# A cross-attention kernel with adapter tokens on one core: another hand-laid order of all operations and another choice of engines

## The chip, the cores and the metric

The kernel runs on one core of a Trainium2 chip. The core has five engines with a queue each: TensorE (PE, matrix products; its weight loads are shown apart as PEld), VectorE (DVE), ScalarE (ACT), GpSimd (POOL) and SyncE (SP), which here issues nearly all DMAs. Each engine works through its queue in program order and waits on semaphores for the others. SBUF holds the working data, PSUM the results of PE in banks. The metric is the device time of one execution in microseconds, from repeated runs.

## The reference

x is 2 x 2048 x 640 in f32, the context 2 x 128 x 384: 124 text keys and T = 4 adapter tokens. With 8 heads of 80:

```python
query = hidden_states @ Wq
keyt = enc @ Wk
valt = enc @ Wv
hs = _mha(query, keyt, valt)
ca_q1 = jnp.einsum('btc,th->bch', ca, Wq_ca)
ca_q1 = ca_q1[:, indices, :]
ca_hs1 = _mha(ca_q1, residual, residual)
ca_q2 = ca_hs1 @ Wq
ca_k2 = ca @ Wk_ca
ca_v2 = ca @ Wv_ca
ca_hs2 = _mha(ca_q2, ca_k2, ca_v2)
out = hs + ca_hs2
out = out @ Wout + b_out
out = out + residual
```

So there is a text attention over 124 keys, and a second branch that attends from the adapter tokens over all 2048 rows of x (the rows `indices` choose), and once more over the four tokens. Their sum goes through Wout, with bias and residual.

## The kernel before

The rows of x are taken as 8 blocks of 512 (four to a batch entry: `x_load`, `queries`, `yz_block`) and, for the attention, as UNITS = 16 units of two tiles of 128 rows (`text(m)`). For a unit, PE multiplies queries and keys (`sc`), DVE takes the maxima (`m`), ACT the exponentials (`p`) and their sums, POOL or DVE multiplies by the reciprocal sums `r`, DVE transposes in blocks (`eb`), and the result goes out to DRAM (`kept`) and comes back transposed (`pT`); then PE multiplies by the values (`ph`) and by Wout (`po`), and DVE adds the parts to the row tile with bias (`x_more`, `last_rows`), which is stored. Units in BY_SUMS = (0, 1, 2, 3, 4, 6, 7) use f32 products in a form that saves multiplications (`text_out_fast`); the other nine use three f32r products with weights split into a rounded top, a rest and a mixed part (`wout_top`, `wout_low`, `wout_mix`; inputs `ks`).

The adapter branch runs beside this for each of the two batch entries. It first takes maxima over all rows (`s` on PE, 128 x 2048 at a time, and `mx` on DVE), then the exponentials (`ea` on ACT) and the products `acc`; `pt_acc`, `prod`, `s2f`, `p`, `p2t` and `pt_p` are its second softmax over the tokens and what makes of it the weights that join the text probabilities.

A head has 80 columns, and what goes beyond the first 64 of each pair of heads is kept apart as a rest. For the keys (`keys`, L824) the fifth chunk is rounded to f32r and to its rest by ACT (`k_parts<-k_rest`) and DVE, written to DRAM (`k_away`), read back in another layout by four DMAs (marks `krest`) and cast by ACT to `krest`. The score matmuls of the first unit read first `kmain` and `q`, then `krest` and `rests`. The scratch tile of this chain is one of three weight buffers (room `weights`).

What sets the order is neither a scheduler nor the language. Every part of the work is a generator that yields operations (`Do`), each with its allowed engines, the operations it must follow, and the buffers it takes and frees (`Room`). All generators are tasks with a number. `Desk.run` (L190) reads the text table `ORDER` (L75 on) entry by entry: a task's number, and a letter where the engine is chosen (a for ACT, v for DVE, g for POOL). An entry issues the next operation of that task. The order of the table is thus the order in each engine's queue. Semaphore waits follow from the data.

In the profile's rows L221 is the matmul of `Desk`, L225 its warm-up matmul, L229 its transpose, L236 every vector, scalar and GpSimd operation, and L246 every DMA; so rows are told apart by tile names.

Of the kernel before, what the change touches and what calls it, by code (L numbers as in the profile page):

```python
# [14 lines left out]
P = 128  # L15
# [52 lines left out]
class Desk:  # L68
# [12 lines left out]
    158 159v 158 158 158 9 36 160 162v 18 12 36 163a 12 13 36 117 123 158 17 154 158 158 158 154 154 39 161 123
    17 117v 161 165g 154 161 117v 171 175 17 161 166g 161 164 18 164 164 17 18 117g 36 164 117g 154 154 164 117g
    164 161 18 176a 164 36 164g 161 16 36 18 18 167g 171 177 16 164 16 16 16 18 36 178a 117v 117 18 43 16 36 16g
    171 181 161 117g 18 18 180 164 168g 180 36 182a 16 17 180 117g 179 180 36 179 16 171 183 16g 174 185 184a 18
    180 18 180 18 36 172 186 36 174 18 17 17 179 18 179 174 188 170 187 187 19 20 21 161 21 187 187 172 192 187
    20 189 190 21 187 36 43 36 179 179 21 173 203 203 203 191 191 36 193 191 173 204 169 103 203 191 180 36 180g
    203 191 19 21 203 21 194g 180 36 19 200 209 20 21 195g 19 36 19 191 21 39 102 210a 191 19 21 21 36 19 191
    212 200 213 211 19g 205 211 212 17 196g 20 214a 203 19 212 197g 211 212 36 200 215 211 212 180 203g 201 212
    191 20 19 212 21 216a 21 19g 21 36 20 20 21 212g 211 211 21 206 217 217 36 22 23 24 24 202 24 200 218 217
    217 24 206 222 219a 203 217 36 22 223 24 217 203 36 24 47 22 22 22 208 228 226 202 202 22 24 207 229 24 44  # L90
# [159 lines left out]
def kernel(  # L250
# [58 lines left out]
    late = {}  # L309
# [991 lines left out]

    def front_rooms():

        yield Do("NONE", lambda: None, ["late"])
        t = late["pool"].tile([P, 2, 4 * P], F32R, tag="rests", name="rests")
        rest_tiles.extend(t[:, i].rearrange("p (g n) -> p g n", g=4) for i in range(2))
        rests.grow(2)
# [1059 lines left out]
```

## Time and profile before

| | us |
|---|---|
| runs before: median of three (lowest to highest) | 564.55 (564.24 to 566.42) |
| profiled execution, first to last instruction | 562.1 |
| PE busy | 549.2 |
| DVE busy | 402.2 |
| ACT busy | 276.3 |
| POOL busy | 208.1 |

The profile is of one execution. Its span is taken from the first to the last instruction; the time of a run is the whole execution on the device. The page lists busy time by engine and by group of equal instructions; the list of waits says which engine stood idle for what; a table of windows gives busy time in chosen stretches; a timeline has the instructions in order of their start, with the idle time before each in brackets and what ended it. A group's mean is its busy time over its count, and operations on one engine overlap at their edges by some tens of nanoseconds.

### The profile page before, as it was taken

The numbers are of one execution on the slowest core, as the hardware profiler recorded it, in microseconds if no ns is written. First come the engines' busy times: TensorE is split into PE (matmuls) and PEld (weight loads), VectorE is DVE, ScalarE is ACT, GpSimd is POOL, SyncE is SP. The second block draws the span as 40 slices with busy tenths as digits, with TensorE's granted clock in tenths as the row PEclk, the third lists the DMA queues.
The fourth block names the chain that finished last, engine by engine and source line by source line (L and its number), as shares of the span: only waits on it lengthen the run. The fifth ranks groups of instructions, "written<-read, shape, count | busy, mean of one in ns | idle before, by whom it ended". The sixth has DMA issues, their size and how long they took to land.

```text
span 562.1 us, 17332 instructions
## 1 busy us (share of the span) xinstructions
PE 549.2 (98%) x7338; PEld 337.8 (60%) x7338; DVE 402.2 (72%) x621; ACT 276.3 (49%) x752; POOL 208.1 (37%) x206
## 2 busy tenths in 40 slices
PE   9999999999999999999999999999999899999997
PEld 8563455556555655455365445455554477989796
DVE  2457999999996564589999998655735886449542
ACT  3122645445338898886524524589878432111200
POOL 7002625344424522013559364512424830441040
PEclk9999999999999999999999999999999989999999
DMA  8994759774876899446558895859865367977533
GB/s 258 244 175 121 163 123 166 163 159 142 170 199 155 183 251 180 136 160 176 177 126 247 226 232 133 255 149 254 244 172 177 74 124 215 264 215 195 160 123 129
DMA packets 151549, 101.38 MB, mean 180 GB/s; under 512 B 86476, under 2 KB 130012, under 8 KB 151472
## 3 DMA queue, kind: packets, MB, share of 16 engines
q1 hardware_dynamic: 150704, 99.88, 69.5%
q8 instruction: 58, 0.95, 0.8%
q0 software_dynamic: 768, 0.40, 0.4%
q14 instruction: 19, 0.16, 0.1%
HBM read 61.34 MB, written 38.90 MB: 178 GB/s over the span
## 4 chain that ended last, share of the span: by engine, by line
PE 82%; DVE 7%; DMA 5%; ACT 2%; issue 2%; SPq 1%; DVEq 0%; ACTq 0%
PE po L221 23%; PE pq L221 23%; PE acc L221 7%; PE sc L221 6%; PE s L221 6%; PE ph L221 5%; PE pq_first L221 3%; PE pyz L221 3%; DVE mx L236 2%; ACT p L236 1%; DMA bias<-in_L_xattn_b_out_dram 1%; PE pk L221 1%; PE unread L225 1%; ACT ea L236 1%; PE pv L221 1%
## 5 line engine op out<-in xcount | busy, mean ns | idle before, releaser
L236 DVE TENSOR_REDUCE mx<-s 128x4 f32<-128x2048 f32 x48 | 109.2, 2275 | 2.9 <-PE s L221 2.8
L236 POOL TENSOR_TENSOR p<-p,r 128x992 f32<-128x992 f32 x29 | 53.8, 1856 | 141.1 <-DVE r L236 135.0
L236 ACT ACTIVATE ea<-s 128x2048 f32<-128x2048 f32 x48 | 90.4, 1884 | 25.6 <-PE s L221 25.3
L236 ACT ACTIVATE p<-sc,m 128x124 f32<-128x124 f32 x256 | 89.5, 374 | 25.7 <-DVE m L236 25.7
L236 ACT ACTIVATION_READ_ACCUMULATOR p<-sc,m 128x1 f32 x256 | 55.5, 217 | 0.0
L221 PE MATMUL pq<-xt,wq_sb 128*32 128x256 f32 x896 | 54.3, 381 | 0.6 <-DVE q L236 0.6
L236 DVE TENSOR_REDUCE m<-sc 128x4 f32<-128x496 f32 x64 | 40.6, 662 | 13.9 <-PE sc L221 13.7
L221 PE MATMUL acc<-ea,y_sb 128*32 128x384 f32 (+2 forms) x768 | 50.1, 383 | 0.0
L221 PE MATMUL ph<-pT,vpad 128*32 128x256 f32 x768 | 45.8, 380 | 0.8 <-DMA out_dram<-x_more 0.3
L236 DVE STREAM_TRANSPOSE eb<-p 128x1024 f32<-128x1024 f32 x32 | 39.5, 1233 | 4.5 <-POOL p L236 3.3
L221 PEld LDWEIGHTS pq<-xt,wq_sb 128*32 128x32 f32 x896 | 27.5, 110 | 22.9 <-issue 5.5
L221 PEld LDWEIGHTS sc<-kmain,q 64*128 64x128 f32 x512 | 31.8, 187 | 11.6 <-issue 8.4
L221 PE MATMUL pq<-xt,wq 128*32 128x512 f32 x320 | 38.8, 595 | 0.0
L221 PE MATMUL po<-wout_sums,hs 128*32 128x320 f32 x448 | 35.4, 438 | 3.5 <-DVE x_more L236 2.9
L221 PE MATMUL sc<-kmain,q 64*128 64x124 f32 x512 | 37.5, 283 | 0.1
L221 PE MATMUL po<-wout_sb,hs 128*32 128x320 f32 (+1 forms) x452 | 36.4, 434 | 0.7 <-DVE prod L236 0.6
L221 PE MATMUL po<-wout_low,ks 128*128 128x320 f32 x204 | 35.7, 308 | 0.0
L221 PEld LDWEIGHTS ph<-pT,vpad 128*32 128x32 f32 x768 | 24.4, 110 | 18.6 <-issue 2.6
L236 POOL TENSOR_TENSOR last_rows<-last_rows,bias 128x640 f32<-128x640 f32 x10 | 17.0, 1697 | 44.7 <-DMA last_rows<-in_x_dram 44.7
L221 PE MATMUL po<-wout_top,ks 128*128 128x320 f32 x180 | 32.5, 311 | 0.0
L221 PEld LDWEIGHTS acc<-ea,y_sb 128*32 128x32 f32 x768 | 21.1, 109 | 17.3 <-issue 8.6
L221 PEld LDWEIGHTS po<-wout_low,ks 128*128 128x128 f32 x204 | 31.3, 188 | 0.0
(232 smaller groups left out, 951.4 us busy)
## 6 DMA issues: line engine op xcount, KB each, us to landing
kept<-eb SPq DMA_DIRECT2D x32, 512.0 KB
pT<-kept SPq DMA_DIRECT2D x48, 256.0 KB
landing<-away SPq DMA_DIRECT2D x60, 128.0 KB
xi<-in_x_dram SPq DMA_DIRECT2D x28, 256.0 KB
x_more<-in_x_dram SPq DMA_DIRECT2D x17, 320.0 KB
out_dram<-x_more SPq DMA_DIRECT2D x16, 320.0 KB
last_rows<-in_x_dram SPq DMA_DIRECT2D x15, 320.0 KB
out_dram<-last_rows SPq DMA_DIRECT2D x14, 320.0 KB
```

Source lines behind the costliest of these rows:

```text
L221: self.pin(self.nc.tensor.matmul(out[strip], lhsT[:, strip], rhs, **kw))
L225: self.pin(self.nc.tensor.matmul(out, zeros, zeros, start=True, stop=True))
L236: return lambda *args, **kw: self.pin(getattr(engine, what)(*args, **kw))
```

## The change

The whole table `ORDER` is replaced, so that every engine's queue is laid out anew. Of the table, its first two lines of before stand here for all; of the code, the core:

```diff
     ORDER = """
-    2 4 4 0 2 36 0 0 2 0 0 2 0 0 2 0 0 2 0 0 2 2 124 2 4 2 0 128a 0 2 0 6 6 6 2 125 4 6 130a 126 4 131a 127 4 4
-    132a 6 133v 2 3 4 6 3a 2 15 3 6 3a 15 15 3 6 3v 3 7 7 8 8 7 8 11 7 7 15 0 8 135a 0 134a 7 5 8 7 7 15 9 7
...
@@ -2224,6 +2216,25 @@
+    def mixing(mix, top, low, after, marks):
+
+        def first():
+            if desk.engine == "ACT":
+                desk.a_activation(mix(), raw(low()), AF.Identity, scale=UP)
+            else:
+                mixed(mix(), raw(top()), raw(low()))
+
+        op = yield Do(("DVE", "ACT"), first, after)
+
+        def second():
+            if op.ran == "ACT":
+                minus(mix(), raw(top()), raw(mix()))
+
+        yield Do(("NONE", "POOL", "DVE"), second, marks=marks)
...
-    def stored(m, k, u, added):
+    def stored(m, k):
 
         b, st = tiles(m)[k]
-        t, i, _ = xr_of[m][k]
-        cols = slice(*spans[u])
-        yield Do(
-            "SP", lambda: dma(out[b, st * P : (st + 1) * P, cols], t[:, cols]), added,
-            frees=[(rows, i)] if u == 2 else [],
-        )
+        for u in (2,) if m < UNITS - 1 else (0, 1):
...
+            yield Do(
+                "SP", store, added,
+                frees=lambda: [(rows, xr_of[m][k][1])] if u == 2 else [],
+            )
```

The other edits give an operation's buffers free with the operation itself (`frees`, `grows`) rather than in a statement behind it, begin the stores of a unit with the unit, and put the two steps of a mixed part into one helper. The stores and the operations are the same ones. Lines move up by five: the matmul is L216 and the vector operations L231 in the change.

PE does the same products. On the other engines, counting instructions: DVE 607 to 617, ACT 498 to 503, POOL 211 to 203, SP's DMAs 427 in both. Among what changes engine: the multiplication of `p` by `r` (POOL 29 to 20, DVE 3 to 12), the subtractions that make `wout_low` (DVE 4 to 0, POOL 1 to 5), some additions for `x_sums` (POOL 24 to 20, DVE 4 to 8) and those of the bias (POOL 21 to 18).

First place: ACT's queue in the setup, ahead of the first exponentials. `k_parts<-k_rest` is the first step of the chain of the keys' rest, `krest<-k_parts` its last; the `vpad` copies take the products `pv` of the values from PSUM. Before:

```order
L236 ACTIVATE cop<-ca_150,low_c 128x384
L236 CAST k_parts<-k_rest 128x248
L236 ACTIVATE yz_0_509<-pyz_0_0_510,ones 128x512
...
L236 COPY vca<-pvca 128x2x64
L236 COPY vca<-pvca 128x16 x2
L236 COPY vpad_107<-pv_0_620 124x4x64
L236 COPY vpad_107<-pv_0_620 124x2x16 x2
L236 CAST krest<-k_parts 128x992
L236 COPY vpad_108<-pv_1_693 124x4x64
L236 COPY vpad_108<-pv_1_693 124x2x16 x2
L236 CAST rests<-first_rests 128x512 x2
```

and now:

```order
L231 COPY vca<-pvca 128x2x64
L231 COPY vca<-pvca 128x16 x2
L231 COPY vpad_107<-pv_1_653 124x4x64
L231 COPY vpad_107<-pv_1_653 124x2x16 x2
L231 CAST k_parts<-k_rest 128x248
L231 CAST krest<-k_parts 128x992
L231 COPY vpad_108<-pv_1_708 124x4x64
L231 COPY vpad_108<-pv_1_708 124x2x16 x2
L231 CAST rests<-first_rests 128x512 x2
```

The first step, which had many rows between it and the last, now stands right ahead of it, behind the copies of `pv_1_653`. On PE that product is the third from last of the values; behind it come `pv_0_667`, one `s`, `pv_1_708`, one `s`, the `kmain` half of the first scores and then their `krest` half, as in before.

The same chain in SP's queue, before:

```order
L246 DMA wout_sb<-in_L_xattn_Wout_dram 64x4x640
L246 DMA k_away<-k_parts 128x2x248 x2
L246 DMA k_parts<-k_away 32x4x248
L246 DMA away_618<-first_rests 256x1x256
L246 DMA v_638<-vca 128x192
L246 DMA k_parts<-k_away 32x4x248 x3
L246 DMA first_rests<-away_618 32x4x256 x4
```

and now:

```order
L241 DMA away_476<-first_rests 256x1x256
L241 DMA first_rests<-away_476 32x4x256 x4
L241 DMA k_away<-k_parts 128x2x248 x2
L241 DMA xi_2_553<-in_x_dram 32x64x32
L241 DMA xi_2_553<-in_x_dram 32x16x16 x2
L241 DMA k_parts<-k_away 32x4x248 x2
L241 DMA v_616<-vca 128x192
L241 DMA k_parts<-k_away 32x4x248 x2
```

The rests of the first queries now go out and come back ahead of the keys' chain, and three loads of x stand between its write and its reads.

Second place: DVE's queue behind `prod` of the second batch entry, ahead of the last phase. Before:

```order
L236 TENSOR_TENSOR prod<-pt_acc_1_5786,r_1_1_5790 128x3x96
L236 TENSOR_TENSOR wout_low<-wout_sb,wout_top_5736 128x640
L236 TENSOR_TENSOR wout_low<-wout_sb,wout_top_5694 128x640
L236 TENSOR_TENSOR wout_low<-wout_sb,wout_top_5690 128x640
L236 TENSOR_TENSOR wout_low<-wout_sb,wout_top_5692 128x640
L236 TENSOR_TENSOR wout_mix_5827<-wout_top_5694,wout_low 128x640
L236 TENSOR_TENSOR wout_mix_5828<-wout_top_5735,wout_low 128x640
L236 TENSOR_REDUCE s2f<-prod 128x8x3 x3
L236 TENSOR_REDUCE m_1_5837<-s2f 128x24
L236 TENSOR_TENSOR p_1_5732<-s2f,m_1_5837 128x96
L236 TENSOR_TENSOR x_more<-x_more,po_1_5840 128x320
```

and now:

```order
L231 TENSOR_TENSOR prod<-pt_acc_1_5747,r_1_1_5751 128x3x96
L231 TENSOR_REDUCE s2f<-prod 128x8x3 x3
L231 TENSOR_REDUCE m_1_5785<-s2f 128x24
L231 TENSOR_TENSOR p_1_5698<-s2f,m_1_5785 128x96
L231 TENSOR_REDUCE r_1_5700<-p_1_5698 128x24
L231 RECIPROCAL r_1_5700<-r_1_5700 128x24
L231 TENSOR_TENSOR p2t_5699<-p_1_5698,r_1_5700 128x3x8x4
L231 TENSOR_REDUCE m_15_0_5818<-sc_15_0_5800 128x4
L231 TENSOR_REDUCE m_15_1_5819<-sc_15_1_5801 128x4
L231 TENSOR_REDUCE m_14_0_5775<-sc_14_0_5757 128x4
L231 TENSOR_SCALAR ks_5821<-ph_2_5836 128x512
```

The splits of Wout (`wout_low`, `wout_mix`) are gone from between `prod` and `s2f`. The five subtractions stand in POOL's queue, behind the masks of the token rows, and DVE's four mixes come some ten rows further on than what is shown.

More of the change, by code (lines that the diff above doesn't have):

```diff
@@ L81 @@
[L81 to L90, printed above, removed]
@@ L1302, in front_rooms @@
     def front_rooms():
[L1304 removed]
+        yield Do("NONE", lambda: None, ["late"], grows=[(rests, 2), (landing, 1)])
         t = late["pool"].tile([P, 2, 4 * P], F32R, tag="rests", name="rests")
         rest_tiles.extend(t[:, i].rearrange("p (g n) -> p g n", g=4) for i in range(2))
[L1307 removed]
         landing.tile = late["pool"].tile([P, 4, 2 * P], F32, tag="landing", name="landing")
[L1309 to L1310 removed]
+        yield Do("NONE", lambda: None, [("rest", 0, i) for i in range(2)], grows=[(sums, 1), (halves[0], 1)])
         t = xrow.tile([P, 2 * P * NCH * 2], F32, tag="xr", name="x_sums")
@@ L1575, in scores @@
                     return q4, ea_tile(e[0], f"ea_{b}_{j}_{v}", 512), e[0]
-                op = yield Do("PE", scores, [("cop", b)], needs=[(quad, 1), (eas, 1)])
+                st = pieces(v)[-1][0]
+                ends_ = j == 1 and 512 * (v + 1) == CAD * (st + 1) and st % 4 == 3
+                op = yield Do(
+                    "PE", scores, [("cop", b)], needs=[(quad, 1), (eas, 1)],
+                    frees=(lambda st=st: [(zops, room_of["zop", b, st // 4])]) if ends_ else (),
+                )
                 q4, e, i = op.value
@@ L1587, in adapter @@
                 if j == 1 and 512 * (v + 1) == CAD * (st + 1) and st % 4 == 3:
-                    zops.give(room_of["zop", b, st // 4])
+                    late["ps_"]=0
         yield Fork(second(b))
@@ L2188, in add @@
                     desk.v_tensor_tensor(t, t, po[:, :HALF], ALU.add)
-                op = yield Do("DVE", add, [op.at], frees=[(banks, s)] if end else [])
+                op = yield Do(
+                    "DVE", add, [op.at], frees=[(banks, s)] if end else [], marks=[("added", m, i, n, k)],
+                )
                 at = [op.at]
-                key = (m, i, 2)
-                ends.setdefault(key, []).append(op.at)
-                if len(ends[key]) == 4:
-                    yield Fork(stored(*key, ends[key]))
         for n, steps in enumerate(chains):
@@ L2237, in hidden_parts @@
         )
-        def scaled():
-            if desk.engine == "ACT":
-                desk.a_activation(cols("mix"), cols("low", True), AF.Identity, scale=UP)
-            else:
-                mixed(cols("mix"), cols("top", True), cols("low", True))
-        op = yield Do(("DVE", "ACT"), scaled)
-        both = op.ran == "ACT"
-        yield Do(
-            ADDS if both else "NONE", lambda: both and minus(cols("mix"), cols("top", True), cols("mix", True)),
-            marks=[("hs mix", m, c0)],
-        )
+        yield from mixing(lambda: cols("mix"), lambda: cols("top"), lambda: cols("low"), [("hs low", m, c0)], [("hs mix", m, c0)])
     def out_part(m, i, u, hs):
@@ L2304, in text @@
         yield Fork(probabilities(m))
+        for k in range(2):
+            yield Fork(stored(m, k))
     begin = desk.begin
```

174 lines of the change are left out of this document (86 added, 88 removed), and 7 rows, old and new, of the table ORDER.

## The prediction

> **What bounds the kernel now.** I read the page first, then the list of what TensorE (PE) waits for, then a table by stage, and last the timelines at the two places where the new order differs most.
>
> ```profile
> span 562.1 us, 17332 instructions
> PE 549.2 (98%) x7338; PEld 337.8 (60%) x7338; DVE 402.2 (72%) x621; ACT 276.3 (49%) x752; POOL 208.1 (37%) x206
> ```
>
> The columns are busy us, share of the span and count. PE is busy for 98% of the span, so no reordering can win much unless it also removes matmuls, and this one removes none. All that an order can win is PE's idle time, 562.1 - 549.2 = 12.9 us, and what a lowered clock costs. The next list says where the larger part of it is (target of the wait, us in all, times, longest).
>
> ```profile
> PE po L221 <- DVE x_more L236: 2.9, 1, 2.9
> PE s L221 <- DVE mx L236: 1.1, 2, 0.8
> PE po L221 <- DVE prod L236: 0.6, 1, 0.6
> ```
>
> One wait of 2.9 us stands out; the others are fractions of a microsecond, spread over the program. The stages show how near the next engine is to PE:
>
> ```profile
> 57.00:165.00 108.00, 107.23 (x1644) 58.69 (x1648) 102.88 (x127) 52.56 (x206) 48.41 (x38) 1.00 0.74 162
> 165.00:260.00 95.00, 94.82 (x1439) 51.31 (x1427) 59.90 (x98) 81.03 (x186) 28.32 (x24) 1.00 0.71 172
> 260.00:335.00 75.00, 72.77 (x1031) 37.75 (x1031) 72.13 (x78) 31.81 (x121) 43.35 (x38) 1.00 0.75 200
> 335.00:430.00 95.00, 94.37 (x1477) 51.68 (x1473) 57.94 (x97) 68.19 (x151) 29.68 (x22) 1.00 0.70 196
> 430.00:455.00 25.00, 21.48 (x313) 11.13 (x307) 21.13 (x32) 13.92 (x21) 21.89 (x18) 0.93 0.53 131
> ```
>
> After the stretch and its length come the busy us of PE, weight loads, DVE, ACT and POOL, then the granted clock. DVE is nearly full in 57 to 165 (102.88 of 108) and 260 to 335 (72.13 of 75), ACT in 165 to 260 (81.03 of 95). The one stage where PE loses much is 430 to 455: 21.48 of 25 us busy, at a mean clock of 0.93. Its end, and the setup before 57, are where I expect the change to act.
>
> **The change, part by part.** The working starts from the profiled execution. The measured runs' median of 564.55 us is 2.45 us above its span of 562.1; I carry that difference over unchanged.
>
> *First place: the drain before the last phase.* In the order of before, DVE does the Wout splits ahead of the adapter's second softmax:
>
> ```profile
> 439.29 0.46 DVE L236 TENSOR_TENSOR prod<-pt_acc,r 128x288 f32<-128x288 f32 x1
> 439.66 5.51 DVE L236 TENSOR_TENSOR wout_low<-wout_sb,wout_top 128x640 fp32r<-128x640 f32 x4
> 445.10 2.10 DVE L236 TENSOR_TENSOR wout_mix<-wout_top,wout_low 128x640 fp32r<-128x640 f32 x2
> 447.13 1.66 DVE L236 TENSOR_REDUCE s2f<-prod 128x24 f32<-128x192 f32 x3
> 449.29 0.47 DVE L236 TENSOR_TENSOR x_more<-x_more,po 128x320 f32<-128x320 f32 x1
> 451.30 1.07 DVE L236 TENSOR_TENSOR p2t<-p,r 128x96 f32<-128x96 f32 x1
> ...
> 438.91 1.16 PE L221 MATMUL sc<-kmain,q 64*128 64x124 f32 x16
> 440.40 1.28 PE L221 MATMUL po<-wout_sums,hs 128*32 128x320 f32 x16
> 441.50 1.05 PE L221 MATMUL ph<-pT,vpad 128*32 128x256 f32 x16
> 449.82 1.66 PE L221 MATMUL po<-wout_sums,hs 128*32 128x320 f32 x16 [2.85 <-DVE x_more L236]
> 453.04 1.52 PE L221 MATMUL pt_p<-rows,p2t 128*32 128x512 f32 x12 [0.49 <-DVE ks L236]
> ...
> 450.60:454.00 3.40, 2.91 (x25) 1.18 (x20) 3.30 (x7) 0.95 (x3) 3.32 (x2) 0.50 0.73 153
> ```
>
> The PSUM bank that `po` needs is freed by the x_more addition, and that stands behind 5.51 + 2.10 + 1.66 us of other DVE work. PE idles 2.85 us, then 0.49 us more, and in 450.60 to 454.00 it runs at a clock of 0.50: 2.91 us of busy time do 1.45 us of work. The place loses 2.85 + 0.49 + 1.45 = 4.8 us. In the changed order `wout_low` is no longer on DVE (five subtractions go to POOL), the mixes come later, and s2f to p2t follow `prod` at once. p2t then comes, behind the end of `pt_acc` at 438.98, 0.8 us later with `prod` (439.75), and then the 1.66 us of s2f, the 1.07 of p2t and four small steps of about 0.26 each: 4.6 us. In the changed order PE has two score products and two `ph` between `pt_acc` and `pt_p`; one score product takes 440.40 - 438.91 = 1.49 us here and one `ph` at most 1.05, so 2 x 1.49 + 2 x 1.05 = 5.1 us at most. The two are about even, and no `po` stands behind the splits: the long wait goes. What is late next: `pt_p` (up to 0.7 us), the matmuls behind ACT's copy of `rows` (0.5), and two `po` that wait for `ks` (0.3), 1.5 us together. None reaches 2.85 us, so the clock should stay. **Gain 4.8 - 1.5 = 3.3 us**, between 1 (if the new waits come to 3.8: one of the old size, 2.85, and one more) and 4.8.
>
> *Second place: the rest of the keys in the setup.* This speaks against the change. The rounded rest of K is written to DRAM and read back in another layout (k_parts to k_away to k_parts), then cast to `krest`, which the score matmuls read:
>
> ```profile
> 38.00 0.40 ACT L236 CAST k_parts<-k_rest 128x248 fp32r<-128x248 f32 x1 [5.36 <-PE pk L221]
> 41.61 0.40 DVE L236 TENSOR_TENSOR k_parts<-k_rest,k_parts 128x248 fp32r<-128x248 f32 x1
> 42.07 1.07 SPq L246 DMA_DIRECT2D k_away<-k_parts  x2
> 45.28 0.32 SPq L246 DMA_DIRECT2D k_parts<-k_away  x1
> 51.03 0.48 SPq L246 DMA_DIRECT2D v<-vca  x1
> 51.56 1.42 SPq L246 DMA_DIRECT2D k_parts<-k_away  x3
> 51.61 0.55 ACT L236 COPY vpad<-pv 124x256 f32<-124x256 f32 x3 [0.64 <-PE pv L221]
> 56.43 1.02 ACT L236 CAST krest<-k_parts 128x992 fp32r<-128x992 f32 x1 [4.28 <-DMA k_parts<-k_away]
> 57.36 0.54 ACT L236 COPY vpad<-pv 124x256 f32<-124x256 f32 x3
> 58.25 1.14 ACT L236 CAST rests<-first_rests 128x512 fp32r<-128x512 f32 x2 [0.35 <-DMA first_rests<-away]
> ...
> 49.66 5.05 PE L221 MATMUL pv<-w_v,ctxT 128*32 128x320 f32 x72
> 57.72 0.50 PE L221 MATMUL s<-zop,cop 32*128 32x512 f32 x4 [0.82 <-DVE mx L236]
> 59.07 0.65 PE L221 MATMUL sc<-krest,rests 64*128 64x124 f32 x8
> ```
>
> In before the chain starts with the cast at 38.00, 21 us ahead of its user at 59.07, and no time is lost. In the changed order that cast stands on ACT behind the copies of the third `pv` from the end, so it cannot start before PE has finished that product. That is the second of the three in the row at 49.66, so it ends at 49.66 + 2 x 5.05 / 3 = 53.0. From there PE's program is the same as before up to the `krest` half, which before took 59.07 - 53.0 = 6.1 us, with the 0.82 us wait for `mx` in it. The new chain from the same instant: copies 0.55, cast 0.40, subtraction 0.40, write to first read 45.28 - 42.07 = 3.21, the issues of four reads and the `v` load among them 0.32 + 1.42 + 0.48 = 2.2, last issue's end to cast 56.43 - 52.98 = 3.45 (52.98 is 51.56 + 1.42), krest 1.02, copies 0.54, first half of rests 0.57. Sum 12.3 us. **PE waits 12.3 - 6.1 = 6.2 us.** Little runs beside it: DVE can do one more `mx` and then stands at an operand sum whose buffer the same chain frees, and SP is in order. The bounds: if a read lands as the write does, 45.28 - 43.14 = 2.14 us behind the last issue and not 3.45, and the one `mx` (2.28 us, below) is won back later in a stage where DVE is the fuller engine, 6.2 - 1.3 - 2.3 = 2.6 (the write's second issue ends at 42.07 + 1.07 = 43.14); if the x loads now issued between write and read (three, and in before two such cost SP 4.69 us) hold the reads up by one of them, 6.2 + 2.3 = 8.5.
>
> ```profile
> 60.91 2.28 DVE L236 TENSOR_REDUCE mx<-s 128x4 f32<-128x2048 f32 x1
> 28.43 4.69 SPq L246 DMA_DIRECT2D xi<-in_x_dram  x2
> ```
>
> The clock is a cost of its own here. Behind the 2.85 us wait it was 0.50 for 3.4 us and 1.45 us of work was lost; a wait twice as long should bring the same, but DVE gets the lost time as a lead in a stage where it is short. I take 0.7, with 0 and 1.45 as ends. The Trainium skill, page "TensorE: Matmul & The Clock Gate", section "Part 1: The HAM clock gate", says that one idle window of about 3.4 us puts the clock to half until a busy window has passed, and that the window runs freely. By it a wait of 6.2 us cannot escape, and the sum would be some 0.8 us higher. The trace agrees as to the stretch (3.4 us at 0.50), though here a wait shorter than a window sufficed. For the read-back the skill's "DMA: Bandwidth & Descriptors", "Anatomy of one DMA", gives about 2.0 us fixed cost; with it twice, in place of the two row-based landings, the sum would be about 1.6 us lower. The landings of 2.14 and 3.45 us here decide.
>
> *Third: engines changed elsewhere.* Nine more `p` multiplications run on DVE instead of POOL.
>
> ```profile
> L236 POOL TENSOR_TENSOR p<-p,r 128x992 f32<-128x992 f32 x29 | 53.8, 1856 | 141.1 <-DVE r L236 135.0
> L236 DVE TENSOR_TENSOR p<-p,r 128x992 f32<-128x992 f32 x3 | 3.5, 1180 | 0.0
> L236 DVE TENSOR_TENSOR wout_low<-wout_sb,wout_top x4: 812/1372/2192, 439.7 to 443.0; 128x640 fp32r<-128x640 f32 x4
> ```
>
> They add 9 x 1.18 = 10.6 us to DVE and take 9 x 1.86 = 16.7 from POOL, nearly all within the stages 165 to 260 and 335 to 430, where DVE is idle for 35 and 37 us. Neither is on PE's path, so I count nothing; were that cover gone, each would cost its 1.18. The last row shows DVE's same subtraction taking 0.81 to 2.19 us while POOL works: the two engines hold each other up. Fewer of these beside POOL's large operations may help in 260 to 335, where PE loses 75 - 72.77 = 2.2 us. The stage 57 to 165 gets a little more for DVE to do (one more addition for `x_sums` and one for `zop`, from POOL) with only 5 us of room. I take -1.0 for both stages together, between +1 and -2.5 (all of 260 to 335 and some of the rest). The stores begun under other marks, the rooms freed inside the operation and the common `mixing` helper issue the same DMAs and vector operations; nothing.
>
> Sum: 562.1 + 6.2 + 0.7 - 3.3 - 1.0 = 564.7; with 2.45 around it **567.2 us**.
>
> **Rivals.** (a) *The setup wait is absorbed and the change wins.* If DVE sets the pace in 57 to 165, PE's loss at `krest` is only what DVE loses: the chain of 2.6 with no clock loss. With the full gain of the drain and of the lock, 562.1 + 2.6 - 4.8 - 2.5 = 557.4, or 560 us. For it: DVE's 102.88 of 108. Against: PE is 107.23 of 108 there, so it has no lead to give. It decides where the wait at `krest` is below 3.5 us. (b) *The setup is worse.* Reads behind x loads, full clock loss and nothing won by the lock: 562.1 + 8.5 + 1.45 - 2 = 570, or 572.5 us. For it: SP's order and DVE's fullness behind the wait, which then runs late against `mx` again. (c) *It evens out.* The chain costs 3.5 us with little clock loss, and drain plus lock win 3.5 to 4: about 564.5 us. That the order isn't what the table says is no rival, as the operations stand in it one by one.
>
> **How the numbers follow.** The forecast, that the setup wait is about 6 us and is not made good: 0.45. (a) 0.2, (b) 0.2, (c) 0.15. The range takes in (a) and (b) but for their outer tails: 559.5 to 573. A measurement of this kernel can tell about 0.5% from no change, 561.7 to 567.4. Faster: (a), 0.2. Slower: (b) and somewhat under half of the forecast, 0.4. Same: the rest, 0.4.
>
> **What would show it.** In the changed profile PE should have one wait of 4 to 8 us at `sc<-krest` near 60 us, with ACT's krest cast idle on the read of k_parts, and the granted clock near 0.5 behind it; the row for 430 to 455 should have no wait above 1 us and a clock of 1.00. If the first wait is under 3 us the chain was sized wrongly; if the last phase still begins with a 3 us wait, the drain was; if PE loses over 3 us in 57 to 165 behind the setup, it is DVE that was misjudged.

## The result, and the profile after

| | before | after |
|---|---|---|
| runs: median (lowest to highest) | 564.89 us (564.24 to 566.42) | 571.9 us (571.36 to 572.58) |
| profiled execution, first to last instruction | 562.1 us | 570.6 us |
| mean granted TensorE clock in it | 0.997 | 0.990 |

The ratio is 1.0109, with a 95% interval of 1.007 to 1.0149: the new order is slower by about 1%. (The quotient of the two medians is 1.0124, inside the interval; in the table of the experiments too the ratio need not be the quotient of the medians beside it.) Forecast were 567.2 us, with 559.5 to 573 as the range. The page of the changed kernel (busy us, share, count; then TensorE's clock in 40 slices, in tenths):

```profile
span 570.6 us, 17331 instructions
PE 550.6 (97%) x7350; PEld 337.3 (59%) x7350; DVE 408.6 (72%) x631; ACT 279.1 (49%) x757; POOL 184.6 (32%) x198
PEclk9999699999999999999999999999999999999999
```

PE's idle time is 570.6 - 550.6 = 20.0 us, where it was 12.9, and one slice, the fifth (57 to 71 us), has a low clock. The list of PE's waits (target, us in all, times, longest) says where the idle time is:

```profile
PE sc L216 <- ACT rests L231: 6.3, 1, 6.3
PE pt_p L216 <- DVE wq_sums L231: 2.0, 1, 2.0
PE pt_p L216 <- DVE p2t L231: 1.4, 1, 1.4
PE po L216 <- DVE ks L231: 0.8, 1, 0.8
```

The first is the wait that the prediction put behind the keys' chain. The third and fourth are in the drain, where a wait of 2.85 us for `x_more` is gone. The second is new, and the prediction had nothing of it. The table by stage (busy us of PE, weight loads, DVE, ACT, POOL; clock):

```profile
57.00:165.00 108.00, 100.69 (x1468) 53.94 (x1464) 95.68 (x117) 49.35 (x191) 44.41 (x37) 0.95 0.81 180
269.50:344.50 75.00, 71.74 (x1020) 37.72 (x1016) 71.02 (x79) 31.84 (x110) 37.98 (x34) 1.00 0.73 192
438.50:463.50 25.00, 22.64 (x351) 12.56 (x347) 19.53 (x33) 13.75 (x31) 21.19 (x19) 1.00 0.58 131
60.90:66.20 5.30, 0.00 (x0) 0.00 (x0) 1.27 (x3) 2.03 (x6) 0.18 (x2) 0.50 1.04 206
66.20:71.10 4.90, 4.90 (x44) 2.59 (x44) 3.05 (x5) 0.61 (x2) 4.35 (x5) 0.50 1.12 135
```

The second and third rows are those of the prediction for 260 to 335 and 430 to 455, taken 9.5 and 8.5 us later, where the same work lies now (`pt_acc` of the second batch entry starts at 446.92 us in place of 438.43). PE is idle for 7.3 us in 57 to 165 (0.8 in before) and for 3.3 in the second row (2.2). The drain improved: 2.4 us idle against 3.5, and no half clock. The last two rows are the first wait and what follows it: the clock fell to half within the wait, at 60.9 us, and stayed there until 71.1; behind the wait PE is busy throughout, at half clock.

**The setup**, in the timeline of the changed kernel (start, us, engine, operation; in brackets the idle time before it and what ended it):

```profile
53.78 0.55 ACT L231 COPY vpad<-pv 124x256 f32<-124x256 f32 x3 [4.72 <-PE pv L216]
54.20 0.42 ACT L231 CAST k_parts<-k_rest 128x248 fp32r<-128x248 f32 x1
55.13 0.89 SPq L241 DMA_DIRECT2D k_away<-k_parts  x2
56.07 2.77 SPq L241 DMA_DIRECT2D xi<-in_x_dram  x3
59.02 0.83 SPq L241 DMA_DIRECT2D k_parts<-k_away  x2
64.17 1.02 ACT L231 CAST krest<-k_parts 128x992 fp32r<-128x992 f32 x1 [9.54 <-DMA k_parts<-k_away]
65.22 0.42 DVE L231 TENSOR_TENSOR wq_sums<-wq_sb 128x256 f32<-128x256 f32 x1 [4.03 <-ACT krest L231]
58.77 1.16 PE L216 MATMUL sc<-kmain,q 64*128 64x124 f32 x16
66.20 1.11 PE L216 MATMUL sc<-krest,rests 64*128 64x124 f32 x8 [6.27 <-ACT rests L231]
67.25 3.64 PE L216 MATMUL pq<-xt,wq_sb 128*32 128x256 f32 x32
70.82 0.65 PE L216 MATMUL s<-zop,cop 32*128 32x512 f32 x4
```

From the copies' start to the `krest` product it is 66.20 - 53.78 = 12.4 us, as summed (12.3), and PE waits 6.27. DVE stands 4.03 us for the buffer that this chain frees. Behind the wait, three products take 1.11, 3.64 and 0.65 us; the second experiment, which keeps the clock at full there, has 0.66, 1.93 and 0.50 for the same three. The half clock costs 2.3 us by that; half of the 4.90 us in the last row above, 2.45, is near it.

**The second softmax of the first batch entry** is where the unforeseen wait is:

```profile
293.71 2.28 DVE L231 TENSOR_REDUCE mx<-s 128x4 f32<-128x2048 f32 x1
297.99 0.30 ACT L231 ACTIVATE p<-p 128x96 f32<-128x96 f32 x1
298.20 1.84 POOL L231 TENSOR_TENSOR p<-p,r 128x992 f32<-128x992 f32 x1
298.94 1.29 DVE L231 TENSOR_TENSOR p2t<-p,r 128x96 f32<-128x96 f32 x1
300.64 1.08 PE L216 MATMUL pt_p<-rows,p2t 128*32 128x512 f32 x12 [1.98 <-DVE wq_sums L231]
```

ACT's short exponential stands behind seven other operations, so DVE's `p2t` starts only at 298.94, and then it takes 1.29 us. In before the same `p2t` took 0.34 us, with POOL idle:

```profile
287.31 0.34 DVE L236 TENSOR_TENSOR p2t<-p,r 128x96 f32<-128x96 f32 x1
```

Here POOL's multiplication of two SBUF tensors runs from 298.20 to 300.04 and `p2t` ends at 300.23, just behind it. The Trainium skill, page "SBUF — State Buffer", section "SBUF: two separate sides", says that DVE with two SBUF inputs and a GpSimd operation that reads SBUF share one pair of ports under an exclusive lock, so that the later one waits out the earlier. This trace agrees. (PE's wait is put down to `wq_sums`, the last DVE instruction that overlaps; it is `p2t` that PE needs.) The 1.98 us are those of one execution: in the profiles of the experiments that keep this order (e1, e2, e4 and e8) the same wait is 0.57 to 1.21 us, and in e8 1.21 with a `p2t` of only 0.33.

**The drain**, with PE and DVE of the second batch entry:

```profile
451.65 8.07 POOL L231 TENSOR_TENSOR wout_low<-wout_sb,wout_top 128x640 fp32r<-128x640 f32 x5
451.93 1.45 DVE L231 TENSOR_TENSOR p2t<-p,r 128x96 f32<-128x96 f32 x1
453.51 1.08 PE L216 MATMUL pt_p<-rows,p2t 128*32 128x512 f32 x12 [1.36 <-DVE p2t L231]
458.96 1.28 PE L216 MATMUL po<-wout_sums,hs 128*32 128x320 f32 x16 [0.81 <-DVE ks L231]
```

`p2t` is slowed again, now by the first of the `wout_low` subtractions that moved to POOL. The new waits come to 1.36 + 0.81 = 2.2 us.

All of it is in one account. I put PE's matmuls of each kernel in a row, gave each its full-clock duration, and took how far its start lies behind their sum. The difference to before, by the work that PE has done:

| work done, us | 50 | 60 | 160 | 270 | 280 | 300 | 410 | 420 | end |
|---|---|---|---|---|---|---|---|---|---|
| after, us later than before | 0.4 | 9.1 | 10.5 | 9.5 | 12.6 | 11.3 | 11.6 | 9.2 | 8.5 |

Nearly all is lost at one place, between 50 and 60: 8.7 us, of which 6.27 + 2.3 = 8.6 are the wait and the clock. The drain (410 to 420) gives 2.4 back, and 270 to 280 takes 3.1.

### The profile page after: what moved, and what is told of

It is laid out like the page before. It is cut to its first block, busy times and chain, and to the rows that moved or that the text cites. A ratio compares the mean times of both kernels' runs of the same rounds, so it can differ in the third digit from the quotient of the medians.

```text
span 570.6 us, 17331 instructions
## 1 busy us (share of the span) xinstructions
PE 550.6 (97%) x7350; PEld 337.3 (59%) x7350; DVE 408.6 (72%) x631; ACT 279.1 (49%) x757; POOL 184.6 (32%) x198
## 4 chain that ended last, share of the span: by engine, by line
PE 71%; DVE 12%; ACT 5%; DMA 4%; issue 3%; POOL 2%; SPq 1%; ACTq 0%; DVEq 0%; POOLq 0%
PE po L216 21%; PE pq L216 20%; PE acc L216 6%; PE sc L216 6%; PE s L216 6%; PE ph L216 5%; DVE mx L231 5%; ACT ea L231 3%; PE pyz L216 2%; PE pq_first L216 2%; SPq L241 1%; DMA ca<-in_ctx_dram 1%; DVE eb L231 1%; DVE m L231 1%; DVE x_more L231 1%
## 5 line engine op out<-in xcount | busy, mean ns | idle before, releaser
L231 DVE TENSOR_REDUCE mx<-s 128x4 f32<-128x2048 f32 x48 | 109.4, 2279 | 4.8 <-PE s L216 4.4
L231 ACT ACTIVATE p<-sc,m 128x124 f32<-128x124 f32 x256 | 90.0, 377 | 34.7 <-DVE m L231 33.9
L231 ACT ACTIVATE ea<-s 128x2048 f32<-128x2048 f32 x48 | 90.5, 1886 | 20.6 <-PE s L216 20.4
L231 POOL TENSOR_TENSOR p<-p,r 128x992 f32<-128x992 f32 x20 | 37.6, 1880 | 71.0 <-DVE r L231 71.0
L216 PE MATMUL pq<-xt,wq_sb 128*32 128x256 f32 (+1 forms) x872 | 56.3, 390 | 0.0
L231 ACT ACTIVATION_READ_ACCUMULATOR p<-sc,m 128x1 f32 x256 | 56.0, 219 | 0.0
L216 PE MATMUL acc<-ea,y_sb 128*32 128x384 f32 (+2 forms) x768 | 50.7, 383 | 0.2 <-ACT ea L231 0.2
L231 DVE TENSOR_REDUCE m<-sc 128x4 f32<-128x496 f32 x64 | 40.7, 661 | 12.8 <-PE sc L216 12.8
L216 PE MATMUL ph<-pT,vpad 128*32 128x256 f32 x768 | 46.0, 381 | 0.4 <-issue 0.4
L231 DVE STREAM_TRANSPOSE eb<-p 128x1024 f32<-128x1024 f32 x32 | 39.5, 1236 | 6.5 <-DMA kept<-eb 4.4
L216 PEld LDWEIGHTS pq<-xt,wq_sb 128*32 128x32 f32 (+1 forms) x872 | 28.8, 112 | 20.8 <-issue 6.3
L216 PE MATMUL pq<-xt,wq 128*32 128x512 f32 (+1 forms) x284 | 39.0, 596 | 0.0
L216 PE MATMUL sc<-kmain,q 64*128 64x124 f32 x512 | 37.4, 284 | 0.0
L216 PEld LDWEIGHTS sc<-kmain,q 64*128 64x128 f32 x512 | 31.4, 187 | 9.8 <-issue 7.0
L216 PE MATMUL po<-wout_sums,hs 128*32 128x320 f32 x448 | 35.3, 434 | 0.8 <-DVE ks L231 0.8
L216 PE MATMUL po<-wout_sb,hs 128*32 128x320 f32 (+1 forms) x452 | 36.0, 434 | 0.0
L216 PE MATMUL po<-wout_low,ks 128*128 128x320 f32 x204 | 35.7, 308 | 0.0
L216 PEld LDWEIGHTS ph<-pT,vpad 128*32 128x32 f32 x768 | 23.6, 110 | 17.7 <-issue 2.7
L216 PE MATMUL po<-wout_top,ks 128*128 128x320 f32 x180 | 32.4, 310 | 0.0
L216 PEld LDWEIGHTS po<-wout_low,ks 128*128 128x128 f32 x204 | 31.3, 188 | 0.0
L216 PEld LDWEIGHTS acc<-ea,y_sb 128*32 128x32 f32 x768 | 20.9, 109 | 17.6 <-issue 8.9
L231 ACT ACTIVATE ks<-ph 128x512 fp32r<-128x512 f32 (+1 forms) x13 | 6.8, 529 | 48.5 <-PE ph L216 48.5
```

Of the source, the lines that this page charges most:

```text
L216: self.pin(self.nc.tensor.matmul(out[strip], lhsT[:, strip], rhs, **kw))
L231: return lambda *args, **kw: self.pin(getattr(engine, what)(*args, **kw))
```

## The experiments

In the diffs, a row of a queue is one instruction, with buffer numbers left out; they show what stands where in the named queue. The kernels are told by the number in their label (none has the number 7), and each was compared with the kernel before on the same chip. "Before" below is its median there.

| label | edit | median us | before | ratio, 95% interval |
|---|---|---|---|---|
| e1_krest_early | chain early | 567.2 | 566.47 | 1.0019 [0.9999, 1.0039] |
| e2_zero_fill | wait filled | 569.43 | 566.47 | 1.0061 [1.004, 1.0082] |
| e3_before_late | before, chain late | 573.52 | 566.47 | 1.0132 [1.0092, 1.0172] |
| e4_xi_behind | x loads behind the reads | 571.0 | 566.47 | 1.009 [1.0055, 1.0125] |
| e5_before_drain | before, p2t ahead of splits | 566.18 | 565.52 | 1.0002 [0.9975, 1.0028] |
| e6_share_early | first p2t earlier | 570.99 | 565.52 | 1.0101 [1.0066, 1.0135] |
| e8_krest_early2 | e1, two more places | 567.65 | 565.52 | 1.0045 [1.0022, 1.0068] |
| e9_both | e8 and e6 | 565.5 | 565.52 | 1.0002 [0.9982, 1.0021] |
| e10_away_early | e9, rests' write early | 565.11 | 566.14 | 1.0002 [0.9983, 1.0022] |
| e11_lock_free | e10, POOL idle at p2t | 565.26 | 566.14 | 0.9991 [0.9968, 1.0014] |
| e12_mx_first | e11, mx ahead of xi_2 | 562.5 | 565.48 | 0.9946 [0.9934, 0.9959] |

**The chain's place.** In the first experiment the chain of the keys' rest begins as soon as its buffer is free, on all queues:

```diff
 ACT:  ACTIVATE zop<-zs,low_z
+ACT:  CAST k_parts<-k_rest
 ACT:  COPY vca<-pvca
 ACT:  COPY vpad<-pv_1
-ACT:  CAST k_parts<-k_rest
 ACT:  CAST krest<-k_parts
 SP:   DMA k_away<-k_parts x2
+SP:   DMA k_parts<-k_away x4
 SP:   DMA xi<-in_x_dram x3
-SP:   DMA k_parts<-k_away x2
 SP:   DMA v<-vca
-SP:   DMA k_parts<-k_away x2
```

> The changed kernel, but the chain of the keys' rest begins as soon as its scratch buffer is free, behind the pvca product: the cast ahead of the vca copies on ACT, the subtraction ahead of the mx of the first maximum on DVE, and on SP the write and the four reads ahead of the x loads. All else stands. Theory (the krest wait of 6.3 us and the half clock behind it, 2.3 us, are the loss): the write is issued near 49.5 instead of 55.1 us, the wait at sc<-krest falls below 0.6 us, the granted clock stays 1.00, and the time is 571.9 - 6.3 - 2.3 = 563.3 us (562.3 to 564.5). Rival (DVE sets the pace in 57 to 165, so that PE's gain is lost again to waits for mx): 567 to 570 us, with new waits for mx between 60 and 165. Rival (the loss lies elsewhere): 571 to 572.

The wait for the chain went and the ratio with it, from 1.0109 to 1.0019. But the time stayed 4 us above the expected 563.3, and three things were not as expected, all in its timeline and windows:

```profile
48.47 1.28 POOL L235 TENSOR_TENSOR zop<-zop,zs 128x512 fp32r<-128x512 f32 x1 [35.98 <-ACT zop L235]
48.71 1.32 DVE L235 TENSOR_TENSOR k_parts<-k_rest,k_parts 128x248 fp32r<-128x248 f32 x1 [1.08 <-ACT k_parts L235]
61.45 0.66 PE L220 MATMUL sc<-krest,rests 64*128 64x124 f32 x8 [0.59 <-ACT rests L235]
58.00:62.00 4.00, 2.59 (x36) 1.68 (x28) 3.39 (x2) 2.45 (x6) 0.18 (x2) 1.00 0.92 143
62.00:65.40 3.40, 3.40 (x35) 1.38 (x32) 1.31 (x4) 0.00 (x0) 1.54 (x2) 0.51 0.96 175
```

The chain's subtraction, 0.40 us in the kernel before, took 1.32 beside POOL's addition, and made the `mx` behind it late. `rests` now started behind the `v` load, which had stayed behind the x loads. And the clock fell to half although PE's longest idle time there was 0.82 us: in the 4 us ahead of the fall PE was busy for 2.59. That fall isn't what kept the median up: in seven of the ten executions the mean granted clock is 1.000, and the profiled one, with 0.997, is the fastest of all (565.65 us).

**The clock by itself.** In the second experiment, 26 products with a matrix of zeros are added to the two score tiles during the wait (52 instructions in the profile).

```diff
+                if m == 0 and k == 0:
+                    for z in range(26):
+                        desk.pin(nc.tensor.matmul(
+                            sc[z % 2][:, :NK], late["zeros"], late["zeros"][:, :NK],
+                            start=False, stop=False, skip_group_check=True,
+                        ))
```

> The changed kernel with 26 products of zeros added to the first scores between their kmain half and their krest half (they add exactly zero), some 26 x 0.21 = 5.5 us of PE work in the place where PE idles 6.3 us. Nothing else changes. Theory (the clock falls because PE stands idle, and costs 2.3 us by itself): the krest half starts at the same time, near 66.2, the granted clock behind it is 1.00, and the time is 571.9 - 2.3 = 569.6 us (569.0 to 570.3). Rival (DVE takes the lost PE time as a lead, as the prediction's 0.7 us had it): 571.2. Rival (the clock falls for another reason): 571.9.

The setup of that kernel, in its timeline:

```profile
60.31 6.07 PE L1782 MATMUL sc<-zeros 128*128 128x124 f32 x52
67.13 0.66 PE L216 MATMUL sc<-krest,rests 64*128 64x124 f32 x8 [0.75 <-ACT rests L231]
67.72 1.93 PE L216 MATMUL pq<-xt,wq_sb 128*32 128x256 f32 x32
```

The chain is as late as in the change, but its followers run at full speed, and the clock stays at 1.00 all through. So the half clock behind the wait is a cost of its own, 2.3 us at its place. The span is 567.5, 3.1 us below that of the change, and no lead of DVE's makes the clock's loss good. Not all of the 3.1 is the clock, as the wait at the first `pt_p` is 0.57 us here and was 1.98; and the intervals of the two ratios, 1.0061 and 1.0109, overlap. The rows show the 2.3 more safely than the time does.

**The late chain alone.** The third puts the late chain into the kernel before. Besides, the copies of one values' product move from DVE to ACT, so that the cast can stand behind them:

```diff
-ACT:  CAST k_parts<-k_rest
 ACT:  ACTIVATE yz<-pyz,ones
...
 ACT:  COPY vpad<-pv
+ACT:  CAST k_parts<-k_rest
 ACT:  CAST krest<-k_parts
```

> The kernel before, with only the chain of the keys' rest late as in the change: its cast on ACT behind the copies of the second of the three values' products (which go to ACT for it), the subtraction, the write and the reads behind that, the reads of the first rests ahead of it. No x loads stand between write and reads. Theory: PE waits 5.4 us for krest (6.3 less the x loads' 0.9) and runs at half clock for 2.3 us more: 564.9 + 7.7 = 572.6 us (571 to 574). Rival (only the new order's fuller DVE in 57 to 165 makes the loss stick; the old order absorbs a part): 567 to 570.

Its timeline shows the same wait (in brackets):

```profile
65.34 1.12 PE L217 MATMUL sc<-krest,rests 64*128 64x124 f32 x8 [5.46 <-ACT rests L232]
```

The span is 571.7, 9.6 above before, and in the account of PE's work the difference is 8.2 at 60, 9.2 from 70 to 250 and 9.6 at the end. Nothing is absorbed. The late chain alone costs the old order 1.3% [0.9, 1.7], as much as the whole change. The wait is shorter than in the change and the loss is not, because more of the half clock lies behind it: from 65.34 to 71.63, 6.29 us, where it was 4.90.

**What the loads of x add.** The fourth moves the three x loads behind the four reads:

```diff
 SP:   DMA k_away<-k_parts x2
-SP:   DMA xi<-in_x_dram x3
 SP:   DMA k_parts<-k_away x2
 SP:   DMA v<-vca
 SP:   DMA k_parts<-k_away x2
+SP:   DMA xi<-in_x_dram x3
```

> The changed kernel with the three x loads that stand between the write of the keys' rest and its reads moved behind the reads on SP. Theory (they cost only what their issue lasts beyond the write's landing: 59.02 - (56.02 + 2.14) = 0.9 us): the krest wait is 5.4 us and the time 571.0 us. Rival (their traffic holds the reads up, as the prediction's upper bound had it, by 2.3 us or more): wait below 4 us, time below 569.6. Rival (nothing): 571.9.

```profile
65.00 1.11 PE L216 MATMUL sc<-krest,rests 64*128 64x124 f32 x8 [5.43 <-DMA xi<-in_x_dram]
```

The wait is 5.43 us in place of 6.27. (Its releaser is named by the event that came last; the chain is the same.) The loads cost 0.84 of the wait, not the 2.3 that was the upper bound. The time shows nothing of it (1.009 against 1.0109): in the profiled execution the half clock lasts from the wait's end to 71.41, 6.41 us of PE's work in place of 4.90, and that alone costs 0.75 more.

**The drain by order alone.** The fifth gives the kernel before the change's order on DVE there, with its engines as they were (the few rows of ACT and PE that go with it move too):

```diff
 DVE:  TENSOR_TENSOR prod<-pt_acc,r
+DVE:  TENSOR_REDUCE s2f<-prod x3
+DVE:  TENSOR_TENSOR p<-s2f,m
+DVE:  TENSOR_TENSOR p2t<-p,r
 DVE:  TENSOR_TENSOR wout_low<-wout_sb,wout_top x4
-DVE:  TENSOR_TENSOR wout_mix<-wout_top,wout_low x2
-DVE:  TENSOR_REDUCE s2f<-prod x3
-DVE:  TENSOR_TENSOR p<-s2f,m
-DVE:  TENSOR_TENSOR p2t<-p,r
...
+DVE:  TENSOR_TENSOR wout_mix<-wout_top,wout_low x3
```

> The kernel before, with the drain alone laid out as in the change: on DVE s2f to p2t directly behind prod, one wout_low, then the x_more addition that frees the bank, then the other three wout_low, and the three wout_mix behind the first ks. Engines as before. Theory (the old order of these few operations costs 2.85 + 0.49 us of PE waits and 1.45 us at half clock, of which small new waits for ks take back 1 to 2): no PE wait above 1.5 us between 440 and 460, clock 1.00, and a ratio to before of 0.993 to 0.995 (3 to 4 us). Rival (the splits are due just as soon, so that the wait moves to the first po of wout_low and wout_mix behind 460): ratio 0.999 to 1.001, with a wait of 2 to 4 us there.

```profile
PE pt_p L217 <- POOL rows L232: 2.3, 2, 1.4
PE po L217 <- DVE ks L232: 0.5, 1, 0.5
430.00:455.00 25.00, 22.51 (x327) 11.85 (x323) 19.51 (x30) 13.31 (x17) 19.10 (x17) 0.94 0.51 131
```

The wait for `x_more` went, and `pt_p` waited for POOL's masks instead; the clock fell all the same in this execution (mean 0.995, the lowest of its twelve), and the ratio is 1.0002. In the changed kernel POOL makes the masks in one go ahead of its Wout work; DVE's order alone wins nothing that can be measured.

**The unforeseen wait.** The sixth moves ACT's exponential and DVE's `r` and `p2t` of the first batch entry forward in the changed kernel:

```diff
+ACT:  ACTIVATE p<-p
 ACT:  ACTIVATE zop<-zb,low_z
...
 ACT:  COPY q<-pq
-ACT:  ACTIVATE p<-p
```

> The changed kernel, with the second softmax of the first batch entry earlier: its exponential on ACT ahead of the zop activation and five copies, its sums and p2t on DVE ahead of the x_sums subtraction. Nothing else. Theory (the new PE wait of 2.0 us at pt_p near 300 us is the order of these entries): that wait is gone and the time falls by 2.0 us, to a ratio to before of 1.007 (1.0109 less 2.0 / 565). Rival (DVE is full in 260 to 335, so its other results come later by as much and PE waits for mx instead): the time falls by less than 0.7 us.

The wait of 2.0 us was gone, but the span was only 0.7 us less (569.9), and 1.0101 cannot be told from 1.0109. The rest did not come back as waits: PE's idle time fell from 20.0 to 18.2 us, but its busy time rose from 550.6 to 551.7. Of that 1.1 us, 0.7 is the half clock behind the `krest` wait, which lasted for 6.28 us of PE's work here (65.83 to 72.11) and for 4.90 in the change. So this run does not say what the order is worth; the ninth says more.

**One late transfer behind another.** The eighth takes the first and mends two of its faults: the `v` load ahead of the x loads, and the second addition of `zop` on DVE, so that POOL does not hold up the chain. The ninth adds the sixth's edit.

```diff
 DVE:  STREAM_SHUFFLE zs<-yz
+DVE:  TENSOR_TENSOR zop<-zop,zs
 DVE:  TENSOR_TENSOR k_parts<-k_rest,k_parts
-POOL: TENSOR_TENSOR zop<-zop,zs
 SP:   DMA k_parts<-k_away x4
+SP:   DMA v<-vca
 SP:   DMA xi<-in_x_dram x3
-SP:   DMA v<-vca
```

> As e1_krest_early, with two things mended that its trace shows: the v load goes ahead of the x loads (the cast of rests waited for it), and the second zop addition runs on DVE instead of POOL, so that POOL is idle while DVE subtracts for k_parts (0.40 us in the change, 1.32 us in e1 beside POOL's addition). Theory (the granted clock falls when PE stands idle for a good part of a few microseconds, also in several short waits: in e1 it fell behind waits of 0.82 and 0.59 us and cost 1.6 us): the krest wait is below 0.2 us, the wait for mx ahead of it 0.82, the subtraction takes 0.40, the clock stays 1.00, and the span is 560.5 to 562.0 us, 9 us below the change's 570.6; ratio to before 0.997 to 1.000. Rival (the clock falls there in any case): a stretch of 0.5 near 62 us and a span 1.6 us longer, 562 to 563.5.

> e8_krest_early2 with e6_share_early's order for the second softmax as well. Theory (the changed order is the better one but for these two places): the gains add up, span 558.5 to 560.5 us, ratio to before 0.993 to 0.997. Rival (a gain at the first place only moves DVE's shortage to the second): no lower than e8.

`krest` was no longer waited for in either, and still neither beat before. The two mends of the eighth won nothing that can be measured (1.0045 against 1.0019 of the first). The sixth's edit, which showed nothing by itself, takes the ratio from 1.0045 to 1.0002 on the same chip, with intervals that just do not touch. The profile of the eighth is of its slowest execution, 572.88 us, so the ninth's is read here. Its timeline has a new wait:

```profile
59.28 1.44 SPq L245 DMA_DIRECT2D away<-first_rests  x1
63.92 1.28 POOL L235 TENSOR_TENSOR x_sums<-xt 128x512 f32<-128x512 f32 x1 [4.98 <-ACT q L235]
65.23 1.20 DVE L235 TENSOR_TENSOR x_sums<-xt,x_sums 128x512 f32<-128x512 f32 x1 [2.37 <-POOL x_sums L235]
67.06 2.69 PE L220 MATMUL pq<-x_sums,wq_sums 128*32 128x256 f32 x32 [1.86 <-DVE m L235]
```

The write of the first rests to `away` stood behind the x loads as well. Its buffer is one of those that `x_sums` takes next, so POOL, DVE and then PE stood one behind the other. (The row names ACT as the releaser of POOL; in the first experiment's timeline the same operation stands 2.62 us for `DMA away<-first_rests`.) In the changed kernel all this lay hidden behind the wait for `krest`. The tenth issues that write ahead of the chain's:

```diff
+SP:   DMA away<-first_rests
 SP:   DMA k_away<-k_parts x2
...
 SP:   DMA xi<-in_x_dram x3
-SP:   DMA away<-first_rests
```

> e9_both, with one more DMA moved: the write of the first rests' second half (away<-first_rests), which on SP stood behind four x loads, goes ahead of the write of the keys' rest. Theory (behind the late krest stood a second late transfer: POOL's first x_sums needs the buffer that this write reads, DVE's x_sums needs POOL's, and DVE's m, which frees PE's bank, stands behind it; e9 shows it as 1.86 us at pq and a half clock behind, 1.7 us): both are gone, clock 1.00 between 60 and 75, the span is 563.7 - 1.9 - 1.7 = 560.1 us (559.5 to 561), ratio to before 0.993 to 0.997. Rival (POOL waits for something else, or DVE is simply full): span above 562.5, with a wait of 1 to 2 us near 64.

That wait went too, and a third took its place: PE waited 1.57 us at 73.8 for `mx`. (The profiled execution took 567.97 us, where the median is 565.11.) The ratio stayed at 1.0002, so this mend too won nothing by itself.

**The lock.** The eleventh keeps POOL idle while `p2t` of the second batch entry runs: one `wout_low` goes to DVE, right behind `p2t`, and POOL begins its own with a later part.

```diff
 DVE:  TENSOR_TENSOR p2t<-p,r
+DVE:  TENSOR_TENSOR wout_low<-wout_sb,wout_top
-POOL: TENSOR_TENSOR wout_low<-wout_sb,wout_top x5
+POOL: TENSOR_TENSOR wout_low<-wout_sb,wout_top x4
```

> e10_away_early, with POOL idle while DVE makes p2t of the second batch entry: one wout_low (top 4) runs on DVE behind p2t, and POOL begins with the one whose top ACT makes only behind pt_p. Theory (DVE's two-input operations from SBUF are held up by POOL's: p2t took 0.33 us with POOL idle in e5, 1.07 in before and 1.45 in the change): p2t takes 0.33 to 0.45 us, the PE wait at pt_p falls from 1.4 to below 0.4, and the span is 1.0 us below e10's. Rival (pt_p waits for POOL's masks or for ACT as soon as p2t is early): the wait stays above 0.8 us. Rival (the later splits on POOL hold up the first po of the last phase): the span is no lower than e10's, with a new wait behind 465.

```profile
444.07 0.33 DVE L235 TENSOR_TENSOR p2t<-p,r 128x96 f32<-128x96 f32 x1
444.55 1.08 PE L220 MATMUL pt_p<-rows,p2t 128*32 128x512 f32 x12 [0.25 <-DVE p2t L235]
68.99 0.71 DVE L235 STREAM_TRANSPOSE xt<-xi 128x512 f32<-128x512 f32 x1 [4.04 <-DMA xi<-in_x_dram]
```

`p2t` takes 0.33 us in place of 1.45, with the same data, and PE's wait falls from 1.36 to 0.25. The time doesn't show it: 0.9991 cannot be told from 1.0002. The last row is the cause of the third wait: DVE stands 4.04 us for the loads of `xi_2`, and the `mx` that PE needs stands behind those transposes. The last experiment puts it ahead of them:

```diff
+DVE:  TENSOR_REDUCE mx<-s_0_0_2_0
 DVE:  STREAM_TRANSPOSE xt<-xi x5
-DVE:  TENSOR_REDUCE mx<-s_0_0_2_0
```

> All of the eleventh run's edits (label e11_lock_free: the keys' chain, the first rests' write and loads early, the b=0 second softmax earlier, POOL idle during the b=1 transposes) and one more: VectorE makes mx of s_0_0_2_0 ahead of the transposes of xi_2. In that run VectorE stood 4.04 us for the load of xi_2 with that mx behind it, and TensorE waited 1.32 us for the mx at 74 us and some 0.7 more for what followed from it. Theory (the time after is lost to single late transfers, each with one engine's stream stuck behind it): that wait goes, the span is about 560.7 against 562.7, and the ratio to the kernel before is 0.995 to 0.998. Rival (VectorE is too full between 57 and 165 us for the order there to matter; what is gained at 74 us comes back as waits for ks or wq_sums before 165): the wait at 74 us goes and the ratio stays at 0.999 or above.

```profile
span 561.3 us, 17338 instructions
PE s L220 <- DVE mx L235: 2.2, 4, 0.8
59.17 0.51 PE L220 MATMUL s<-zop,cop 32*128 32x512 f32 x4 [0.82 <-DVE mx L235]
57.00:165.00 108.00, 106.95 (x1614) 58.13 (x1608) 103.47 (x123) 54.40 (x212) 47.93 (x38) 1.00 0.84 183
```

No single wait for `mx` is above 0.8 us any more, the clock is 1.00 throughout, and DVE's fullness (103.47 of 108) does not bring the gain back as a wait. The mean clock is at least 0.998 in all of its twelve executions. The ratio is 0.9946 [0.9934, 0.9959]: with its late transfers mended, the second softmax earlier and POOL idle at `p2t`, the new order beats the kernel before by 0.5%. Behind the first experiment only two single steps are clear of the noise, the sixth's edit on top of the eighth and this last one. In the account of PE's work it is 0.8 us ahead of before at the end; it is still 2.6 us behind at 410 and wins 3.0 in the drain. (That account compares two single executions on two chips, the ratio many on one: the twelve of this kernel took 560.97 to 564.13 us.)

## Why the prediction was right, and where it was not

The time came out 4.7 us above the forecast of 567.2, which by itself could not have been told from no change; it lies inside the range because that reached up to rival (b). Step by step:

**What bounds the kernel: right.** PE sets the end, so a microsecond that it loses in the setup is lost for good; the third experiment shows it most plainly. Rival (a), that DVE's pace swallows the wait, falls with it.

**The chain: right in size and place.** 6.2 us forecast, 6.27 measured. That it is so close is luck, as two of its parts were off and cancel: from the write to the first read it took 59.02 - 55.13 = 3.89 us and not 3.21, as three x loads lay between, and the reads landed 2.87 us behind the last issue and not 3.45 (that issue ends at 61.30, the cast starts at 64.17). With 2.0 us for each landing, as the prediction also quotes, the sum would have been 10.7 us; it was 12.4.

**The clock: the term was mis-sized.** I took 0.7 between 0 and 1.45; it was 2.3. The mechanism was right, as the half clock stood behind the wait in both. Two choices were wrong. The first was that a wait twice as long brings the same stretch of 3.4 us. The clock was at half for 10.2 us, from 60.9 to 71.1, three times the 3.4 of before, and as long in the profiles of e3, e4 and e6. Its first half lay inside the wait, where it cost nothing; 4.9 us of it lay behind, all of them full of work (6.3 to 6.4 us in those three, so 2.3 is at the low end). The second was DVE's lead: it gets none worth having, as it stood for 4.03 us itself, for the buffer of the same chain. With the rule that the prediction quotes from the Trainium skill ("TensorE: Matmul & The Clock Gate", "Part 1: The HAM clock gate") the sum would have been 0.8 us higher, which is nearer. That a wait of 6.2 us "cannot escape" by it was too strong, since less than two freely running windows of 3.4 us need not hold a whole idle one. And such a window is not what the traces show: in the first experiment the clock fell without one, and in the change it fell 1 us after the wait began (at 60.9, with the wait from 66.20 - 6.27 = 59.93).

**The drain: right, somewhat less.** -3.3 forecast, -2.4 in the account. The long wait and the half clock went as told, but the sign "no wait above 1 us" was missed. What is late next was 2.2 us and not 1.5: `pt_p` waited 1.36 us, not up to 0.7, because `p2t` took 1.45 and I had carried over 1.07 from before. Both are the lock with POOL; free of it, `p2t` takes 0.33.

**The engines changed elsewhere: this step failed.** I forecast -1.0 for the stages 57 to 165 and 260 to 335, since fewer DVE operations would run beside POOL's. From 60 to 410 the account rises by 11.6 - 9.1 = 2.5 us. The largest part is the new wait of 1.98 us at the first `pt_p` (0.57 to 1.21 in other profiles of this order): an exponential of 0.30 us queued behind seven other operations, and `p2t` made 0.95 us longer by one POOL operation beside it. I summed the lock over the stages by counts, where it acts on single instructions of the one chain that PE waits for. What makes up the 1.4 us between 60 and 160 stays open: outside the setup PE has no wait above 0.2 us there, so it is not in PE's waits.

Together: 1.6 us for the clock, 0.9 for the drain and 3.5 for the stages are 6.0, against 5.9 between the span forecast, 564.7, and 570.6; what is left nearly cancels (0.4 ahead of the setup, 0.2 in it, -0.7 behind the drain). Rival (b) comes within 0.6 us of the median, but of its parts only the clock loss (larger than its 1.45) and the missing gain in the stages were there; the x loads held the reads up by 0.84 us, not by 2.3.

No step of mine saw that `krest` was the first of three late transfers. The write to `away` and the loads of `xi_2` were late behind it, on the same queue, and each showed only when the one ahead was mended. So undoing the one fault that the profile shows, in the first experiment, took the loss from 1.1% to 0.2% and did not yet bring the gain of 0.5% that the last one has.

## What to carry to other kernels

Where one engine is busy for 98%, look in a new order first for a round trip through DRAM whose first step has moved close to its user, and follow its buffer and every load on the same queue, since a late transfer hides the ones behind it. For a wait of several microseconds on TensorE, count the half clock that follows as a second cost, as long as TensorE is busy in it (here 4.9 to 6.4 us of it, or 2.3 to 3.2 us lost). And look at each two-input VectorE operation on the chain that TensorE waits for: what GpSimd runs at that moment decides whether it takes a third of a microsecond or more than one.

## What was not expected of the hardware

The clock can fall without a long wait: in the first experiment the longest idle time was 0.82 us, and PE's busy share over 4 us was 2.59 / 4.00 = 65%. A wait of 0.82 us at the same place, alone, does not do it: the last experiment has it too and shows 1.00 throughout. Nor does PE's busy share alone decide it, as far as the traces have its products: in the eleventh PE was busy for 2.00 of the 3.41 us from 72.61 to 76.02, 59%, and the clock stayed at 1.00 behind it. What decides stays open.

The lock is felt by two-input operations of VectorE and not by its reductions. `p2t` takes 0.33 or 0.34 us with POOL idle and 1.07, 1.29 or 1.45 beside it, the chain's subtraction 0.40 and 1.32. The sums `r` ahead of `p2t`, a reduction with one input in SBUF, took 0.25 us in the changed kernel, inside POOL's multiplication (298.20 to 300.04), and 0.24 in before, with POOL idle:

```profile
298.32 0.25 DVE L231 TENSOR_REDUCE r<-p 128x24 f32<-128x96 f32 x1 [1.11 <-ACT p L231]
286.69 0.24 DVE L236 TENSOR_REDUCE r<-p 128x24 f32<-128x96 f32 x1
```

The reduction `mx`, which reads PSUM, took 2.28 to 2.29 us in every row shown.
